# A build-time list scheduler with other durations, latencies and filler rule, and score maxima in passes of three or four heads

## The chip, the cores and the metric

The kernel runs on one core of one Trainium2 chip. The metric is the device time in microseconds of one execution; medians are over several runs. TensorE is called PE here (PEld is its weight load), VectorE DVE, ScalarE ACT, GpSimd POOL, and SyncE, which issues the DMAs, SP.

## The reference

Four layers work in sequence on x of shape (8, 256, 32, 32), float32. Cut to what matters:

```python
# layer 0: attention, 4 heads of width 32 (values 64), then a gated feed-forward with 8x8 FFTs
attn = softmax(einsum('bhkn,bhkm->bhnm', q, k) * SCALE)           # 1024 x 1024 per head
out  = einsum('bhdm,bhnm->bhdn', v, attn) + dwconv3(v)
x    = x + gamma1 * proj(out);  x = x + gamma2 * edffn(ln(x))
# layer 1: group norm, attention with 8 heads of width 32, small MLP
attn = softmax(einsum('bhdi,bhdj->bhij', q, k) * temp)
# layer 2: quantised bottleneck convolution, its output is a code of 0 to 255
# layer 3: four scan directions of a selective state space model, 512 channels, 16 states
h = h * exp(dt * A) + dt * B_t * u_t;   y = sum_n h * C_t
```

## The kernel before

The program has two stages, one after the other. `phase_a` computes layers 0 to 2 for the eight samples, up to three of them in flight. `phase_b` computes layer 3: 64 blocks (8 samples, 4 directions, 2 halves of 512 positions), in each 16 states, in each 4 chunks of 128 channels.

**The list.** In both stages the order of instructions on the engines is made when the program is built, by the class `_Order`. Each piece of work is a generator, a *strand*, with a rank. It yields either a condition, for which it waits, or one operation, or a list of operations of one engine that go together. `run` computes for the next operation of every strand the time at which it could start (`start`), takes the earliest (the lower rank at equal times), emits it and moves the engine's clock (`free`) on by the operation's assumed cost. The chip never sees these times: they only decide the order in which each engine's queue holds its instructions. Each engine then works its own queue in order, and waits where its data isn't there.

- `_Op` holds the assumed cost of an operation by engine, size and place. `landing` is the assumed time of a DMA.
- `blocks` names the pieces of a tile that an operation reads or writes. A tile with at most 512 elements per partition is cut in pieces of 64, a larger one in pieces of 512. Two operations that touch one piece are taken as dependent, if one of them writes.
- `LATENCY` is added where a result goes from one engine to another.
- `keep_dense` puts fillers in front of a PE operation: bf16 matmuls of a constant `minus` (line 277 of the profile) whose result nobody reads. It wants work of half of the last 3.4 us. Their number is limited by the room up to the time at which the PE operation can start, or up to 0.66 us after PE became free, whichever is later.

All emitted operations carry line 147 (`_Op.emit`) in the profile, so groups are told apart by tile names: `bank` is a PSUM bank of stage one (eight of them), `stats` holds the maxima, `exps` the exponentials of the attention, `da`, `dbu`, `db`, `h`, `py` and `pp` are tiles of stage two.

**The maxima.** The softmax needs the maximum and the sum of each row of scores before the exponentials are multiplied by the values. `maxima` does this for four heads at a time (once per sample in layer 0, twice in layer 1): 8 row tiles `t`, 2 halves `j` of the keys, 4 heads `h`, that is 64 score tiles of 128x512. One *pass* computes some of them: PE multiplies 32-row slices of q and k, one per head, each in its own group of 32 rows of the array and its own bank; then per head DVE reduces the bank to a negated maximum (`least`) and ACT exponentiates it with that bias and accumulates the sum (`sums`). `least` and `sums` are halves of one `stats` tile of 128 columns. Two strands (`MAXIMA`) work on one list of 32 entries, each for heads h and h+1. A strand takes four heads where four banks are free and the entry is that of head 0, and two otherwise.

**Banks.** `may(n)` tells whether n banks may be taken. While some attention is under way (`attending`), banks of other work (`lent`: maxima and projections alike) may be three at most (`OTHERS`).

**The attention proper.** `exponentials` runs for one sample at a time. A step computes the scores of four 128x512 tiles, subtracts the row terms with the `minus` matmuls, exponentiates on ACT, and a second strand multiplies with the values. `SCORES` is the assumed cost of the first list.

**Stage two.** Eight endless strands work side by side: `scales` (ACT, `dbu`), `turns` (PE transposes into `db`), `decays` (ACT exponentials, `da`), `scans` (DVE, `h`), `products` (POOL, times `cb`), `sums` (PE transposes into `py`), `rows` (SP loads of `cb`), `ahead` (the inputs of coming blocks: projections, convolutions, and in `tables` the batches of ACT functions that need another table). `da` has 5 buffers, `db` 3 banks, `h` 6, `cb` 3.

Of the kernel before, what the change touches and what calls it, by code (L numbers as in the profile page):

```python
# [20 lines left out]
F32 = mybir.dt.float32  # L21
U8 = mybir.dt.uint8
BF16 = mybir.dt.bfloat16
AF = mybir.ActivationFunctionType
ALU = mybir.AluOpType
AX = mybir.AxisListType
# [3 lines left out]
P = 128  # L30
# [3 lines left out]
NT = N // P  # L34
HALF = 512
# [64 lines left out]
class _Op:  # L100


    def __init__(self, engine, method, args, kw):
        self.engine, self.method, self.args, self.kw = engine, method, args, kw
        out, ins = args[0], [a for a in (*args[1:], *kw.values()) if isinstance(a, bass.AP)]
        self.reads = {k for a in ins for k in self.blocks(a)}
        self.writes = {k for a in (out, kw.get("accum_out")) if a is not None for k in self.blocks(a)}
        self.landing = 0.0
        n = max(math.prod(a.shape[1:]) for a in (out, *ins)) / 1024
        near = all(a.space == out.space and out.space != PSUM for a in ins)  # L110
        points = sum(math.prod(a.shape[1:]) == 1 for a in ins)
        if engine == "tensor":
            x = kw.get("rhs", ins[0])
            n = math.prod(x.shape[1:]) / 1024
            self.rows = x.shape[0] / P * n * (0.44 if x.dtype != F32 else 1.72)
            move = method == "transpose" or kw.get("is_transpose", False)
            self.cost = max(0.06, (0.22 if x.shape[0] < 20 else 0) + n * (0.96 if move else 0.44 if x.dtype != F32 else 1.76 if n > 0.2 else 2.0))
            self.rows *= 0.5 if move else 1
        elif engine == "vector":
            fast = near and method in ("tensor_scalar", "tensor_copy")  # L120
            both = near and method == "tensor_tensor"
            three = near and method == "scalar_tensor_tensor"
            if method == "tensor_tensor_scan":
                self.cost = 0.03 + 2.15 * n + 0.05 * points
            elif both or three:
                self.cost = 0.04 + 1.5 * n
            elif fast:
                self.cost = 0.04 + 0.9 * n
            else:
                self.cost = 0.05 + 1.09 * n + 0.05 * points  # L130
        elif engine == "scalar":
            self.cost = 0.05 + 0.06 * near + 0.85 * n + 0.093 * points + 0.17 * ("accum_out" in kw)
        elif engine == "gpsimd":
            self.cost = 0.12 + 2.2 * n if method == "tensor_tensor" else 0.07 + (2.0 if out.dtype == BF16 else 1.5) * n
        else:
            self.cost, self.landing = 0.1, 3.0

    @staticmethod
    def blocks(a):
        step = max(1, a.ap[0][0])  # L140
        lo = a.offset % step
        hi = lo + sum((n - 1) * abs(s) for s, n in list(a.ap)[1:])
        unit = 64 if step <= HALF else HALF
        return [(a.name, k) for k in range(lo // unit, hi // unit + 1)]

    def emit(self, nc):
# [37 lines left out]
class _Order:  # L184
# [2 lines left out]

    LATENCY = 0.35  # L190

    def __init__(self, nc):
        self.nc, self.strands, self.n = nc, [], 0
        self.free, self.written, self.read, self.base, self.last = {}, {}, {}, {}, {}
        self.rooms, self.minus, self.way, self.rows, self.fresh = [], None, 0.0, [], {}

    def add(self, rank, strand):
        self.n += 1
# [30 lines left out]

    def put(self, room, t):  # L230
        k = room.of[t.name]
        end = [v[0] for d in (self.written, self.read) for v in d.pop(t.name, {}).values()]
        self.last[room.tag, k] = max(end + [0.0]) + self.LATENCY
        room.put(t)

    def start(self, ops):
        e = ops[0].engine
        t = self.free.get(e, 0.0)
        for o in ops:
            for k in o.reads | o.writes:  # L240
                t = max(t, self.base.get(k[0], 0.0))
                w, by = self.written.get(k[0], {}).get(k, (0.0, e))
                t = max(t, w + (self.LATENCY if by != e else 0.0))
            for k in o.writes:
                w, by = self.read.get(k[0], {}).get(k, (0.0, e))
                t = max(t, w + (self.LATENCY if by != e else 0.0))
        return t

    WINDOW, DENSE, DUMMY = 3.4, 0.5, 0.22

    def keep_dense(self, t, cost, ops):

        work = sum(o.rows for o in ops)
        free, end = self.free.get("tensor", 0.0), t + cost
        self.rows = [r for r in self.rows if r[1] > end - self.WINDOW]
        seen = sum(w * (b - max(a, end - self.WINDOW)) / (b - a) for a, b, w in self.rows)
        n = math.ceil((self.DENSE * self.WINDOW - seen - work * min(1.0, self.WINDOW / cost)) / self.DUMMY)
        n = max(n, math.ceil((t - free - self.DENSE * self.WINDOW) / self.DUMMY))
        if n > 0:
            since, room, k = min(  # L260
                ((self.last.get((r.tag, k), 0.0), j, k) for j, r in enumerate(self.rooms) for k in r.left),
                default=(1e9, 0, 0),
            )
            x = self.fresh.get(ops[0].args[0].name)
            if x is not None and self.base[x.name] < since:
                since, room = self.base[x.name], None
            begin = max(free, since)
            n = min(n, int((max(t, free + 0.66) - begin) / self.DUMMY))
            if since < 1e9 and n > 0:
                if room is not None:  # L270
                    room = self.rooms[room]
                    room.left.remove(k)
                    room.left.insert(0, k)
                    x = room.take()
                rhs = self.minus.unsqueeze(1).to_broadcast([P, 4, P])
                for _ in range(n):
                    self.nc.tensor.matmul(x, lhsT=self.minus, rhs=rhs, start=True, stop=True)  # L277
                if room is not None:
                    room.put(x)
                    self.last[room.tag, k] = begin + n * self.DUMMY + self.LATENCY  # L280
                self.rows.append((begin, begin + n * self.DUMMY, n * self.DUMMY))
                t = max(t, begin + n * self.DUMMY)
        self.rows.append((t, t + cost, work))
        return t

    def run(self):
        while self.strands:
# [12 lines left out]
            cost, ops = s[2]  # L300
            e = ops[0].engine
            if self.rooms and e == "tensor":
                t = self.keep_dense(t, cost, ops)
            for o in ops:
                o.emit(self.nc)
                for k in o.reads:
# [9 lines left out]
def phase_a(ctx, tc, i, col, ident, codes, w_parts):  # L316
# [18 lines left out]
    order = _Order(nc)  # L335
    NBIG, NMID, NLOW = 12, 9, 7
    OTHERS = 3
    MAXIMA, SCORES = 2, 1.12
    GATE = 1
    big = _Room(rooms, "big", NBIG, [P, CC, N])  # L340
    mid = _Room(rooms, "mid", NMID, [P, N])
# [105 lines left out]
    def hs(h):  # L447
        return slice(h * HALF, (h + 1) * HALF)
# [4 lines left out]
    def may(n):  # L453

        return len(bank.left) >= n and (not attending or len(lent) + n <= OTHERS)
# [13 lines left out]
    def back(b):  # L469
        for t in b if isinstance(b, list) else [b]:  # L470
            lent.discard(t.name)
            put(bank, t)
# [110 lines left out]
    def maxima(rank, q, k, rows, done):  # L583

        both = yield from take(stats)
        least, sums = both[:, 0], both[:, 1]
        todo = [(t, j, h) for t in range(NT) for j in range(2) for h in (0, 2)]
        left = [MAXIMA]

        def some():  # L590
            while todo:
                yield lambda: not todo or may(2)
                if not todo:
                    break
                n = 4 if may(4) and not todo[0][2] else 2
                t, j, h = todo.pop(0)
                if n == 4 and todo:
                    todo.pop(0)
                bb = yield from some_banks(n)
                ops = []  # L600
                for e in range(n):
                    r = slice(32 * (h + e), 32 * (h + e) + 32)
                    ops.append(
                        T.matmul(bb[e], lhsT=q[r, t * P : (t + 1) * P], rhs=k[r, hs(j)], start=True, stop=True)
                    )
                yield (0.9, ops)
                for e in range(n):
                    m, s = (x[:, j, t, h + e : h + e + 1] for x in (least, sums))
                    yield V.tensor_reduce(m, bb[e], AX.X, ALU.max, negate=True)
                    yield A.activation(bb[e], bb[e], AF.Exp, bias=m, accum_out=s)  # L610
                    back(bb[e])
            left[0] -= 1

        for _ in range(MAXIMA):
# [491 lines left out]
        def emit(self, nc):  # L1106
            nc.scalar.preload_act_table_set("natural_log_exp_and_others")

    order.rooms, order.minus, order.way = [bank], minus, 0.05
    stage = [0] * B  # L1110

    def sample(b):
# [670 lines left out]
```

## Time and profile before

| | us |
|---|---|
| median of 3 runs | 10249.33 (10241.9 to 10274.5) |
| profiled execution | 10256.65 |
| its span, first to last instruction | 10254.8 |
| PE, PEld busy | 9573.8, 5920.9 |
| DVE, ACT, POOL busy | 7741.9, 8521.2, 6150.3 |
| granted clock of TensorE | 0.977 |

The profile shows one execution. A group of instructions is written as line, engine, operation, written tile <- read tiles, shapes, count; then busy time in us, mean ns of one, and the idle time of the engine just before them with what ended it. The maxima end at 3564 us and the last DMAs of stage one land near 3700 us; the change of stages shows in the table of 40 slices too, where POOL goes from 1 to 4 tenths to 7 and 8. A matmul of float32 leaves two records of PE, a transpose one. Busy PE is wider than the work in it, since the end of a matmul is modelled.

### The profile page before, as it was taken

Reading aid. Unit: us, or ns where it says so; the run is one execution under the profiler, and the core shown is the slowest. Engines: PE = TensorE matmul, PEld = TensorE weight load, DVE = VectorE, ACT = ScalarE, POOL = GpSimd, SP = SyncE. Lnnn points to the kernel's source line nnn. Section 1 sums busy time; section 2 is a strip of 40 time slices with the busy share of each in tenths; the row PEclk is TensorE's granted clock in tenths of the full one; section 3 lists DMA queues with packets and bytes.
Section 4 is the critical chain, followed back from the end, with each engine's and each line's share of the span. In section 5 each row is a group of like instructions: output and inputs, shape, how many; then the busy total and the mean of one; then the engine's idle time right before and its main releaser. Section 6 shows DMA issues by size and latency. Waiting matters only on the chain.

```text
span 10254.8 us, 153646 instructions
## 1 busy us (share of the span) xinstructions
PE 9573.8 (93%) x57349; PEld 5920.9 (58%) x57349; DVE 7741.9 (75%) x8671; ACT 8521.2 (83%) x15873; POOL 6150.3 (60%) x2993
## 2 busy tenths in 40 slices
PE   9999999999999989999999999999999999999998
PEld 3333333333333347777777777777777776777776
DVE  6366557585666448887888888888888888888788
ACT  7867676767666759988998999898999899898898
POOL 1433132242121038877887878787878787787788
PEclk9998999999999999999999999999999999999999
DMA  2100000000000002112111112111111211111111
GB/s 59 30 19 17 21 22 18 17 22 17 17 17 9 17 29 54 52 47 57 44 55 55 47 51 59 44 55 50 54 51 49 55 54 45 59 50 49 55 46 54
DMA packets 219630, 416.06 MB, mean 41 GB/s; under 512 B 25137, under 2 KB 67505, under 8 KB 213762
## 3 DMA queue, kind: packets, MB, share of 16 engines
q1 hardware_dynamic: 218882, 406.24, 13.7%
q8 instruction: 451, 7.39, 0.3%
q14 instruction: 297, 2.43, 0.1%
HBM read 358.43 MB, written 37.22 MB: 39 GB/s over the span
## 4 chain that ended last, share of the span: by engine, by line
ACT 28%; PE 22%; DVE 10%; issue 2%; POOL 1%; DMA 1%; DVEq 0%; SPq 0%; POOLq 0%; ACTq 0%
ACT da L147 11%; ACT dbu L147 10%; PE pp L147 9%; DVE h L147 8%; PE py L147 7%; PE db L147 6%; ACT L147 2%; ACT xs L147 1%; ACT dt L147 1%; DMA wi<-w_in 1%; POOL h L147 1%; ACT L156 1%; DVE ys L147 1%; ACT st L147 1%; ACT z L147 0%
## 5 line engine op out<-in xcount | busy, mean ns | idle before, releaser
L147 POOL TENSOR_TENSOR h<-h,cb 128x1024 f32<-128x1024 f32 x2048 | 4814.7, 2375 | 1013.8 <-DVE h L147 422.9
L147 ACT ACTIVATE da<-dt,am 128x512 f32<-128x512 f32 x4096 | 2863.9, 714 | 506.0 <-DVE h L147 502.0
L147 ACT ACTIVATE dbu<-du,bT 128x512 f32<-128x512 f32 x4096 | 2783.4, 709 | 17.1 <-PE db L147 10.4
L147 DVE TENSOR_TENSOR_SCAN h<-da,db 128x512 f32<-128x512 f32 x2048 | 2342.4, 1202 | 467.1 <-ACT da L147 201.5
L147 DVE TENSOR_TENSOR_SCAN h<-da,st,db 128x512 f32<-128x512 f32 x2048 | 2466.0, 1262 | 224.8 <-ACT da L147 131.3
L147 PE MATMUL db<-ident,dbu 128*128 128x128 f32 x16384 | 2329.7, 276 | 194.7 <-DVE h L147 157.7
L147 PEld LDWEIGHTS db<-ident,dbu 128*128 128x128 f32 x16384 | 1855.6, 141 | 798.8 <-DVE h L147 350.4
L147 PE MATMUL py<-ident,h 128*128 128x128 f32 x16384 | 2099.2, 274 | 95.4 <-POOL h L147 90.0
L147 PEld LDWEIGHTS py<-ident,h 128*128 128x128 f32 x16384 | 1837.4, 141 | 236.4 <-POOL h L147 179.2
L147 DVE TENSOR_REDUCE stats<-bank 128x1 f32<-128x512 f32 x1536 | 987.9, 684 | 655.0 <-PE bank L147 652.2
L147 ACT ACTIVATE bank<-bank,stats 128x512 f32<-128x512 f32 x1536 | 1024.7, 672 | 409.2 <-DVE stats L147 395.3
L147 POOL TENSOR_TENSOR mid<-mid,mid 128x961 f32<-128x961 f32 (+2 forms) x192 | 394.6, 2062 | 1115.5 <-ACT mid L147 591.9
L147 PE MATMUL bank<-big,big 32*128 32x512 f32 x4096 | 928.3, 667 | 15.7 <-ACT bank L147 9.0
L147 ACT ACTIVATE exps<-bank 128x512 f32<-128x512 f32 x1536 | 796.9, 620 | 166.4 <-PE bank L147 158.9
L147 PE MATMUL pp<-xi,cvd 128*128 128x512 f32 x1488 | 692.6, 601 | 1.6 <-DVE ys L147 1.6
L277 PEld LDWEIGHTS <-minus 128*128 128x128 bf16 x2805 | 260.6, 101 | 663.4 <-issue 463.8
L147 DVE SCALAR_TENSOR_TENSOR mid<-mid,cols,mid 128x961 f32<-128x961 f32 (+1 forms) x384 | 595.6, 1551 | 6.1
L277 PE MATMUL bank<-minus 128*128 128x512 bf16 x1749 | 508.5, 414 | 52.5 <-ACT bank L147 41.1
L147 PEld LDWEIGHTS bank<-big,big 32*128 32x128 f32 x4096 | 283.2, 191 | 463.0 <-issue 267.4
L147 PE MATMUL bank<-exps,big 128*32 128x512 f32 (+1 forms) x3072 | 543.8, 613 | 0.3 <-ACT exps L147 0.3
L147 POOL TENSOR_TENSOR tmp<-dt,xs 128x512 f32<-128x512 f32 x256 | 322.6, 1274 | 298.2 <-ACT dt L147 227.0
L147 POOL TENSOR_TENSOR big<-big,mid 128x992 f32<-128x992 f32 (+1 forms) x128 | 324.4, 2542 | 290.1 <-ACT mid L147 287.4
(207 smaller groups left out, 9389.5 us busy)
## 6 DMA issues: line engine op xcount, KB each, us to landing
cb<-c_d SPq DMA_DIRECT2D x1024, 256.0 KB, 3.3
wi<-w_in SPq DMA_DIRECT2D x192, 192.0 KB, 3.6
big<-in_x_dram SPq DMA_DIRECT2D x16, 1024.0 KB, 5.2
kept<-big SPq DMA_DIRECT2D x16, 1024.0 KB, 3.9
big<-kept SPq DMA_DIRECT2D x16, 1024.0 KB, 4.8
xf<-codes SPq DMA_DIRECT2D x48, 256.0 KB, 4.0
big<-big SPq DMA_DIRECT2D x16, 512.0 KB, 6.7
codes<-low SPq DMA_DIRECT2D x32, 256.0 KB, 2.0
```

Source lines behind the costliest of these rows:

```text
L147: return getattr(getattr(nc, self.engine), self.method)(*self.args, **self.kw)
L156: nc.scalar.preload_act_table_set("natural_log_exp_and_others")
L277: self.nc.tensor.matmul(x, lhsT=self.minus, rhs=rhs, start=True, stop=True)
```

## The change

It has four parts. The durations and landing in `_Op` get other constants, and a term for few-row matmuls goes. `blocks` cuts tiles of at most 256 elements per partition in single columns. `LATENCY` becomes a number by engine of the producer. Fillers may only fill the time before the planned start, and a new method `advance` follows windows of 3.4 us: after a window with less than 0.375 of work the list takes PE at half speed, so that the cost of a PE operation depends on when it runs. The maxima become one strand that takes the next three or four of 64 entries of one head each (the remaining ones at the end), instead of two strands with fixed pairs. `SCORES` and the overhead of a list on PE in stage one (`way`) get other values.

```diff
@@ _Op
-            self.rows = x.shape[0] / P * n * (0.44 if x.dtype != F32 else 1.72)
+            self.rows = x.shape[0] / P * n * (0.427 if x.dtype != F32 else 1.707)
             move = method == "transpose" or kw.get("is_transpose", False)
-            self.cost = max(0.06, (0.22 if x.shape[0] < 20 else 0) + n * (0.96 if move else 0.44 if x.dtype != F32 else 1.76 if n > 0.2 else 2.0))
+            self.cost = max(0.05, n * (0.427 if x.dtype != F32 else 0.854 if move else 1.707))
...
             elif both or three:
-                self.cost = 0.04 + 1.5 * n
+                self.cost = 0.04 + 1.53 * n
             elif fast:
-                self.cost = 0.04 + 0.9 * n
+                self.cost = 0.04 + 0.87 * n
             else:
-                self.cost = 0.05 + 1.09 * n + 0.05 * points
+                self.cost = 0.05 + 1.12 * n + 0.06 * min(points, 1)
         elif engine == "scalar":
-            self.cost = 0.05 + 0.06 * near + 0.85 * n + 0.093 * points + 0.17 * ("accum_out" in kw)
+            self.cost = 0.04 + 0.054 * near + 0.852 * n + 0.093 * points + 0.1 * ("accum_out" in kw)
         elif engine == "gpsimd":
-            self.cost = 0.12 + 2.2 * n if method == "tensor_tensor" else 0.07 + (2.0 if out.dtype == BF16 else 1.5) * n
+            self.cost = 0.12 + 2.3 * n if method == "tensor_tensor" else 0.07 + (2.0 if out.dtype == BF16 else 1.5) * n
         else:
-            self.cost, self.landing = 0.1, 3.0
+            self.cost, self.landing = 0.06, 3.6
...
-        unit = 64 if step <= HALF else HALF
+        unit = 1 if step <= 256 else 64 if step <= HALF else HALF
@@ _Order
-    LATENCY = 0.35
+    LATENCY = {"tensor": 0.21, "vector": 0.12, "scalar": 0.14, "gpsimd": 0.1, "sync": 0.06}
...
-                t = max(t, w + (self.LATENCY if by != e else 0.0))
+                t = max(t, w + (self.LATENCY[by] if by != e else 0.0))
...
+    def advance(self, t, cost, work):
+        while True:
+            while self.window < int(t / self.WINDOW + 1e-9):
+                self.half = self.dense < 0.375 * self.WINDOW
+                self.window, self.dense = self.window + 1, 0.0
+            pace = 0.5 if self.half else 1.0
+            end = (self.window + 1) * self.WINDOW
+            part = min(cost, (end - t) * pace)
+            self.dense += work * part / cost if cost else 0.0
+            work -= work * part / cost if cost else 0.0
+            cost -= part
+            t += part / pace
+            if cost < 1e-6:
+                return t
+            t = end + 1e-6
@@ keep_dense
-            n = min(n, int((max(t, free + 0.66) - begin) / self.DUMMY))
+            n = min(n, int((t - begin) / self.DUMMY))
...
-                self.rows.append((begin, begin + n * self.DUMMY, n * self.DUMMY))
-                t = max(t, begin + n * self.DUMMY)
-        self.rows.append((t, t + cost, work))
-        return t
+                done = self.advance(begin, n * self.DUMMY, n * self.DUMMY)
+                self.rows.append((begin, done, n * self.DUMMY))
+                t = max(t, done)
+        end = self.advance(t, cost, work)
+        self.rows.append((t, end, work))
+        return t, end - t
@@ phase_a
-    MAXIMA, SCORES = 2, 1.12
+    MAXIMA, SCORES = 1, 1.29
@@ maxima
-        todo = [(t, j, h) for t in range(NT) for j in range(2) for h in (0, 2)]
+        todo = [(t, j, h) for t in range(NT) for j in range(2) for h in range(4)]
...
-                yield lambda: not todo or may(2)
+                yield lambda: not todo or may(min(3, len(todo)))
                 if not todo:
                     break
-                n = 4 if may(4) and not todo[0][2] else 2
-                t, j, h = todo.pop(0)
-                if n == 4 and todo:
-                    todo.pop(0)
+                n = min(len(todo), 4)
+                while not may(n):
+                    n -= 1
+                n = min(n, 4)
+                take_now, todo[:n] = todo[:n], []
                 bb = yield from some_banks(n)
...
-                yield (0.9, ops)
+                yield (0.96 if n > 2 else 1.06, ops)
...
-    order.rooms, order.minus, order.way = [bank], minus, 0.05
+    order.rooms, order.minus, order.way = [bank], minus, 0.1
```

More of the change, by code (lines that the diff above doesn't have):

```diff
@@ L195, in __init__ @@
         self.rooms, self.minus, self.way, self.rows, self.fresh = [], None, 0.0, [], {}
+        self.window, self.dense, self.half = 0, 0.0, False
     def add(self, rank, strand):
@@ L231, in put @@
         k = room.of[t.name]
-        end = [v[0] for d in (self.written, self.read) for v in d.pop(t.name, {}).values()]
-        self.last[room.tag, k] = max(end + [0.0]) + self.LATENCY
+        end = [v[0] + self.LATENCY[v[1]] for d in (self.written, self.read) for v in d.pop(t.name, {}).values()]
+        self.last[room.tag, k] = max(end + [0.0])
         room.put(t)
@@ L242, in start @@
                 w, by = self.written.get(k[0], {}).get(k, (0.0, e))
-                t = max(t, w + (self.LATENCY if by != e else 0.0))
+                t = max(t, w + (self.LATENCY[by] if by != e else 0.0))
             for k in o.writes:
                 w, by = self.read.get(k[0], {}).get(k, (0.0, e))
-                t = max(t, w + (self.LATENCY if by != e else 0.0))
+                t = max(t, w + (self.LATENCY[by] if by != e else 0.0))
         return t
     WINDOW, DENSE, DUMMY = 3.4, 0.5, 0.22
+    def advance(self, t, cost, work):
[13 more added lines that the diff above has]
+            t = end + 1e-6
     def keep_dense(self, t, cost, ops):
@@ L279, in keep_dense @@
                     room.put(x)
-                    self.last[room.tag, k] = begin + n * self.DUMMY + self.LATENCY
-                self.rows.append((begin, begin + n * self.DUMMY, n * self.DUMMY))
-                t = max(t, begin + n * self.DUMMY)
-        self.rows.append((t, t + cost, work))
-        return t
+                    self.last[room.tag, k] = begin + n * self.DUMMY + self.LATENCY["tensor"]
+                done = self.advance(begin, n * self.DUMMY, n * self.DUMMY)
[4 more added lines that the diff above has]
+        return t, end - t
     def run(self):
@@ L302, in run @@
             if self.rooms and e == "tensor":
-                t = self.keep_dense(t, cost, ops)
+                t, cost = self.keep_dense(t, cost, ops)
             for o in ops:
@@ L591, in some @@
             while todo:
-                yield lambda: not todo or may(2)
+                yield lambda: not todo or may(min(3, len(todo)))
                 if not todo:
                     break
-                n = 4 if may(4) and not todo[0][2] else 2
-                t, j, h = todo.pop(0)
-                if n == 4 and todo:
-                    todo.pop(0)
+                n = min(len(todo), 4)
[3 more added lines that the diff above has]
+                take_now, todo[:n] = todo[:n], []
                 bb = yield from some_banks(n)
                 ops = []
[L601 to L605, printed above, removed]
-                yield (0.9, ops)
[L607 to L611, printed above, removed]
+                for b, (t, j, h) in zip(bb, take_now):
+                    r = slice(32 * h, 32 * h + 32)
+                    ops.append(T.matmul(b, lhsT=q[r, t * P : (t + 1) * P], rhs=k[r, hs(j)], start=True, stop=True))
+                yield (0.96 if n > 2 else 1.06, ops)
+                for b, (t, j, h) in zip(bb, take_now):
+                    m, s = (x[:, j, t, h : h + 1] for x in (least, sums))
+                    yield V.tensor_reduce(m, b, AX.X, ALU.max, negate=True)
+                    yield A.activation(b, b, AF.Exp, bias=m, accum_out=s)
+                    back(b)
             left[0] -= 1
```

## The prediction

> **What bounds the kernel now.** I read the table of stretches first, because the kernel is two programs one after the other: the first 3640 us are the convolution and attention layers (stage one, the only stage with score maxima), the rest is the state-space scan (stage two).
>
> ```profile
> 0.00:3640.00 3640.00, 3455.60 (x15580) 1229.61 (x15581) 2172.65 (x3236) 2630.82 (x5717) 913.44 (x467) 0.94 0.07 21
> 3640.00:10255.00 6615.00, 6118.25 (x41770) 4691.30 (x41768) 5569.25 (x5436) 5890.40 (x10156) 5236.88 (x2526) 1.00 0.18 51
> ```
>
> The columns after the length are PE, weight loads, DVE, ACT, POOL, then the granted clock. In stage one PE is busy 95% of the time, ACT 72%, DVE 60%, and the clock is 0.94. In stage two ACT is busy 89%, DVE 84%, at full clock. So the stages have different limits and must be costed apart. Next the groups of PE by shape in stage one:
>
> ```profile
> L147 PE MATMUL bank<-big,big 32*128 32x512 f32 x4096 | 928.3, 667 | 15.7 <-ACT bank L147 9.0 <-ACT exps L147 4.1 <-DVE big L147 1.6
> L277 PE MATMUL bank<-minus 128*128 128x512 bf16 x1665 | 488.9, 416 | 52.5 <-ACT bank L147 41.1 <-ACT exps L147 4.1 <-DVE low L147 2.7
> L147 PE MATMUL bank<-big 32*128 32x512 f32 x2048 | 459.0, 657 | 14.3 <-DVE big L147 5.0 <-ACT exps L147 3.9 <-ACT bank L147 2.8
> ```
>
> The 32-row score matmuls are the largest work of PE, and 488.9 us of its busy time are fillers (L277) that compute nothing. A score matmul leaves two records. Half of these 6144 records belong to the maxima (1536 heads), half to the attention proper. Without fillers PE is busy about 2970 of 3640 us, 82%. The timeline of PE then shows what a pass costs:
>
> ```profile
> 1207.69 1.14 PE L147 MATMUL bank<-big,big 32*128 32x512 f32 x8
> 1208.76 1.98 PE L147 MATMUL bank<-big,w_qkv 128*128 128x512 f32 x4
> 1210.68 1.13 PE L147 MATMUL bank<-big,big 32*128 32x512 f32 x4
> 1211.74 0.39 PE L277 MATMUL bank<-minus 128*128 128x512 bf16 x1
> 1212.06 1.13 PE L147 MATMUL bank<-big,big 32*128 32x512 f32 x4
> 1213.12 1.98 PE L147 MATMUL bank<-big,w_qkv 128*128 128x512 f32 x4
> ```
>
> Four heads (x8) take 1.14 us, two heads (x4) take 1.13; from the start of either to the start of what follows is 1.06 us. A pass costs the same however many heads are in it. And DVE, beside the attention of the last sample:
>
> ```profile
> 3398.72 1.29 DVE L147 TENSOR_REDUCE stats<-bank 128x1 f32<-128x512 f32 x2 [6.04 <-PE bank L147]
> 3403.97 1.29 DVE L147 TENSOR_REDUCE stats<-bank 128x1 f32<-128x512 f32 x2 [3.97 <-PE bank L147]
> 3411.65 1.29 DVE L147 TENSOR_REDUCE stats<-bank 128x1 f32<-128x512 f32 x2 [6.38 <-PE bank L147]
> ```
>
> Two heads are reduced in 1.29 us, then DVE waits 4 to 6 us for the next pass. The waits of DVE in stage one put 652.2 us on this. For stage two the waits say that ACT and DVE hold each other up:
>
> ```profile
> ACT da L147 <- DVE h L147: 502.0, 421, 4.8
> DVE h L147 <- ACT da L147: 332.8, 69, 7.6
> DVE h L147 <- PE py L147: 180.4, 219, 3.9
> ```
>
> ACT waits 502 us for a scan to give a buffer back, DVE 333 us for the exponential that ACT has late behind its batches of tables, and 180 us behind PE work that was queued ahead.
>
> **What the Trainium skill says.** "TensorE: Matmul & The Clock Gate", section "Part 3: Packing small matmuls — row/col tiling", says that matmuls in different 32-row groups run together, four at 3.07 times the rate; here 1.14 against 1.13 us for twice the heads agrees. "TensorEngine Tiling (Array Packing)", section "PSUM Bottleneck", warns that emptying PSUM becomes the limit afterwards; here it isn't yet, as ACT is at 72%, but one head needs 0.68 us of DVE and 0.67 of ACT after its share of a pass. The page "TensorE: Matmul & The Clock Gate", section "What's actually happening", has the clock at half rate after an idle window of about 3.4 us; the 0.94 above fits short dips.
>
> **The change part by part.**
>
> *Passes.* Counted in the program, the maxima of before are 670 passes of two and 49 of four: 719 passes. After, a pass takes the next three or four heads of the list whatever their place, so it is between 1536/4 = 384 and 1536/3 = 512 passes. Three holds beside attention (at most three lent banks), four otherwise; I take the middle, 448. That removes 719 - 448 = 271 passes of 1.06 us, **287 us** of PE (219 to 355). The reduces and exponentials, 1536 each, stay. With PE occupied 82% by real work and DVE waiting on it, I put all of it on the path.
>
> *The false chain in the order.* The list takes all 64 columns of the minima as one block (unit 64), so it believes that a reduce must wait until the exponential of another head has read its bias, and adds 0.35 us each time. The trace doesn't have that wait (the stats group waits 25.5 us on ACT, all told), so it costs nothing directly, but it spaces the maxima in the order that the queues must follow. After, each column is its own block. Two strands per pass become one: of these the second covered the time in which the first emptied its banks. I set the gain of the one against the loss of the other, at -80 to +80 us, value 0.
>
> *Fillers.* The old rule lets a group of fillers push a ready matmul by up to 0.66 us, the new one not. Replaying the rule on the kernel before, 68 of 474 groups in stage one do so, 100 of 1749 fillers. At 488.9/1665 = 0.294 us each that is **29 us**; the rest stand in gaps that remain. If most of those gaps are only believed (latency 0.35 against 0.1 to 0.2), up to 150 us more; if the clock falls from 0.94 to 0.91 instead, 3% of 2970 us, 89 us are lost. The three together: value 29.
>
> *Costs and latencies, stage one.* SCORES goes from 1.12 to 1.29, against 0.96 + 0.33 us in the trace between the starts of scores, minus and values. This only places other work better; nothing, bounded by 50 us either way, since it sits inside the attention whose PE work is unchanged.
>
> Stage one: 287 + 29 = 316, taken as **-320 us**, from 3640 to 3320. ACT's 2631 us would then be 79% of it, so ACT doesn't stop it yet.
>
> *Stage two.* No instruction is added or removed but fillers (290 us busy, in a stage where PE isn't the bound). The list's durations come nearer: a 128-column transpose 0.12 to 0.107, where four are 0.47 us apart in weight loads; an exponential 0.628 to 0.613, where two follow at 0.61. Work is then queued on PE less far ahead of the scans. The waits at stake are 502 + 333 + 180 us; a tenth of them, minus what new orders put elsewhere, gives **-60 us**. ACT and DVE alternate, so the sum can't be gained twice. Bounds: -220 (ACT from 89% to 92%) and +130 (2% of 6615), since a greedy order can also come out worse with truer numbers.
>
> Queues: SP's loads keep their places relative to their users except where landing 3.6 instead of 3.0 moves them earlier; the next user waits on three buffers of cb, so zero. POOL's order in stage one changes with ACT's; it is at 25% there, and is covered.
>
> Sum: -320 - 60 = -380 us. The profiled execution took 10256.65 us (span 10254.8), 7.3 above the median of 10249.33. From the median: **9870 us**.
>
> **The rivals.** *A, the passes weren't the path.* Each sample's chain of maxima, attention and projections, or ACT, holds stage one; emptied banks come no faster, and only a third of the PE time shows: 316/3 = 105, stage two 0: 10145 us. For it: ACT waits 409.2 us before the maxima's exponentials, mostly for DVE, not PE. Against: DVE's 652.2 us on PE.
>
> *B, starved maxima (the slower side).* Beside attention a pass of three needs all three lent banks at once, so any projection that holds one bank blocks it, where a pass of two let one stand beside it. A projection holds its bank for about 1.98 + 0.6 = 2.6 us (four records and the copy). With half of the heads beside attention there are 768/3 = 256 such passes; the gain of 380 us is gone at 380/256 = 1.5 us of added wait each, on the path. At 2.6 us it is 666 - 380 = +286: 10535 us. For it: one strand only, and no second one to fill in. Against: maxima rank ahead of projections when banks come free, and passes beside attention are 5 to 8 us apart already.
>
> *C, stage two goes the wrong way.* +130 there and -105 in stage one: 10275 us, about even.
>
> *D, the change does less than it says.* Fewer passes, but still 512 of three, and slower clock: 219 - 89 = -130: 10120 us. It goes with A.
>
> **How the numbers follow.** The forecast, with its bounds, has 0.62; A and D 0.22; B 0.08; C 0.08. A change within 0.3% (31 us) is about what this kernel's measurement cannot tell from none. Of C, 0.03 lies within it and 0.05 above; all of B is slower. So faster 0.84, same 0.03, slower 0.13. The low end: 355 + 100 in stage one and 200 in stage two, 655, gives 9595; I take 9600. The upper end takes in A and D and stops at 10200, leaving out B, C and little else.
>
> **What would show it.** Right: PE rows of x6 and x8 in place of x4, 384 to 512 passes, stage one ending near 3320 us, fewer than 1665 fillers, DVE's wait for PE in the stats group well under 652 us, the clock at 0.92 or more. Stage two: ACT's wait for scans under 502 us and a length of 6500 to 6600. Wrong: stage one over 3550 us with DVE waiting 6 us or more for a pass of three (B); PE at 85% with ACT over 80% (A); stage two over 6650 (C).

## The result and the profile after

The changed kernel takes 10080.6 us (median of 4 runs, 10077.1 to 10083.6) against 10259.5 us of the kernel before in the same comparison: ratio 0.9826, 95% interval 0.9807 to 0.9845. It gains 179 us, 1.7%. The forecast was 380 us. The profiled execution has a span of 10079.9 us, 174.9 less than before.

In every kernel of this study I take stage one to end with the last multiplication by the values, which the view of the tile `exps` gives (minimum, median and maximum in ns, then first and last start in us). Of the changed kernel:

```profile
L147 PE MATMUL bank<-exps,big x3072: 592/592/1117, 175.7 to 3481.0; 128*32 128x512 f32 x128, 128*64 128x512 f32 x64
```

That is 3481.0 us; before it was 3635.6. So stage one became 154.6 us shorter (forecast 320), and stage two, 6619.2 before and 6598.9 after, 20.3 us (forecast 60). The table of stretches, columns as before:

```profile
0.00:3485.00 3485.00, 3256.31 (x15144) 1222.19 (x15145) 2255.23 (x3230) 2610.13 (x5722) 942.48 (x472) 0.95 0.07 22
3485.00:10080.00 6595.00, 6066.05 (x41512) 4707.40 (x41632) 5570.53 (x5436) 5901.83 (x10156) 5238.02 (x2526) 0.99 0.17 51
```

In stage one ACT's work (2610 us) is what it was and its share rose to 75%; the clock is 0.95. Stage two has the same work in nearly the same time. PE's groups in stage one:

```profile
L147 PE MATMUL bank<-big,big 32*128 32x512 f32 x4096 | 845.0, 650 | 14.4 <-ACT bank L147 8.4 <-ACT exps L147 3.3 <-ACT low L147 2.2
L147 PE MATMUL bank<-big 32*128 32x512 f32 x2048 | 422.9, 664 | 19.3 <-DVE big L147 8.9 <-ACT exps L147 4.9 <-ACT bank L147 4.3
L295 PE MATMUL bank<-minus 128*128 128x512 bf16 x1230 | 340.3, 403 | 24.3 <-ACT bank L147 14.5 <-ACT low L147 6.8 <-POOL eps L387 1.6
```

The score matmuls lost 119 us of busy time (928.3 + 459.0 before), the fillers (now line 295) 149 us. The group of DVE's reduces:

```profile
L147 DVE TENSOR_REDUCE stats<-bank 128x1 f32<-128x512 f32 x1536 | 972.0, 681 | 400.7 <-PE bank L147 394.2
```

DVE waits 394 us for passes, 258 less than before. The passes themselves, in PE's timeline:

```profile
1343.50 1.13 PE L147 MATMUL bank<-big,big 32*128 32x512 f32 x6
1344.56 5.42 PE L147 MATMUL bank<-big,w_qkv 128*128 128x512 f32 x12
1349.91 1.14 PE L147 MATMUL bank<-big,big 32*128 32x512 f32 x8
1350.98 0.66 PE L147 MATMUL bank<-ident,big 128*128 128x128 f32 x4
1351.47 1.24 PE L295 MATMUL bank<-minus 128*128 128x512 bf16 x5
1352.65 2.03 PE L147 MATMUL bank<-big,big 32*128 32x512 f32 x8
```

Three heads (x6) and four (x8) cost 1.13 and 1.14 us, as two did, but the last pass of four takes 2.03. ACT's timeline beside it tells why:

```profile
1352.59 0.25 ACT L147 ACTIVATION_READ_ACCUMULATOR bank<-bank,stats 128x1 f32 x1
1352.68 0.70 ACT L147 ACTIVATE bank<-bank,stats 128x512 f32<-128x512 f32 x1
1353.25 0.25 ACT L147 ACTIVATION_READ_ACCUMULATOR bank<-bank,stats 128x1 f32 x1
```

ACT is done with two banks of the pass before at 1352.84 and 1353.50; the weight loads of the third and fourth head start at 1352.89 and 1353.55. PE stands in the middle of the pass until each bank is emptied, and what is queued behind it stands too. I call a pass split if its matmuls start in more than two groups (all first records together, then all second ones, are two). Of the 458 passes some 270 are split, of the 719 before some 75. Last, the waits of stage two (who waited <- for whom: us in all, how often, longest):

```profile
ACT da L147 <- DVE h L147: 444.3, 392, 5.6
DVE h L147 <- ACT da L147: 335.2, 70, 6.4
DVE h L147 <- PE py L147: 185.5, 176, 4.3
```

ACT waits 58 us less for scans; DVE waits as before.

### The profile page after: what moved, and what is told of

It reads as the page before. It is cut to its first block, busy times and chain, and to the rows that moved or that the text cites. A ratio compares the mean times of both kernels' runs of the same rounds, so it can differ in the third digit from the quotient of the medians.

```text
span 10079.9 us, 152800 instructions
## 1 busy us (share of the span) xinstructions
PE 9322.4 (92%) x56655; PEld 5929.6 (59%) x56777; DVE 7825.8 (78%) x8666; ACT 8512.0 (84%) x15878; POOL 6180.5 (61%) x2998
## 4 chain that ended last, share of the span: by engine, by line
PE 28%; ACT 22%; DVE 11%; issue 3%; DMA 1%; POOL 1%; DVEq 0%; SPq 0%; POOLq 0%; ACTq 0%
PE pp L147 12%; DVE h L147 9%; ACT da L147 9%; PE py L147 8%; PE db L147 8%; ACT dbu L147 7%; ACT L147 2%; ACT xs L147 2%; ACT dt L147 1%; DMA wi<-w_in 1%; ACT L156 1%; DVE du L147 1%; POOL h L147 1%; ACT st L147 0%; DVE ys L147 0%
## 5 line engine op out<-in xcount | busy, mean ns | idle before, releaser
L147 PE MATMUL db<-ident,dbu 128*128 128x128 f32 x16384 | 2400.5, 278 | 390.2 <-DVE h L147 336.1
L147 PE MATMUL bank<-big,big 32*128 32x512 f32 x4096 | 845.0, 650 | 14.4 <-ACT bank L147 8.4
L147 DVE SCALAR_TENSOR_TENSOR mid<-mid,cols,mid 128x961 f32<-128x961 f32 (+1 forms) x384 | 629.2, 1639 | 5.9
L147 PE MATMUL bank<-exps,big 128*32 128x512 f32 (+1 forms) x3072 | 565.2, 627 | 0.7 <-ACT exps L147 0.6
L147 POOL TENSOR_SCALAR big<-big,ga,gs 128x512 f32<-128x512 f32 x64 | 74.5, 1176 | 750.6 <-DVE gs L147 292.5
L147 POOL TENSOR_TENSOR big<-big,mid 128x961 f32<-128x961 f32 (+1 forms) x128 | 326.2, 2556 | 302.1 <-ACT mid L147 279.9
L295 PEld LDWEIGHTS <-minus 128*128 128x128 bf16 x2233 | 210.0, 101 | 446.7 <-issue 263.2
```

The costliest lines, as they stand in the source:

```text
L147: return getattr(getattr(nc, self.engine), self.method)(*self.args, **self.kw)
```

## The experiments

Each kernel is the changed one (*after*) or the one before with the edit named. Ratios are to the kernel before on the same chip; its median was 10253 to 10276 us there. Stage lengths come from one profiled execution of each kernel. Where an edit leaves a stage as it was, its length moves by 1 to 4 us (e1 and e13 against *after*).

| | edit | median us | ratio (95%) | stage one | stage two |
|---|---|---|---|---|---|
| before | | 10259.5 | 1 | 3635.6 | 6619.2 |
| after | | 10080.6 | 0.9826 (0.9807 to 0.9845) | 3481.0 | 6598.9 |
| e1 | after, maxima in pairs | 10086.5 | 0.9830 (0.9815 to 0.9845) | 3483.3 | 6599.9 |
| e2 | before, maxima in threes and fours | 10220.8 | 0.9961 (0.9945 to 0.9976) | 3596.9 | 6622.4 |
| e3 | after, banks free later | 10076.6 | 0.9819 (0.9800 to 0.9837) | 3485.7 | 6595.4 |
| e4 | after, old filler rule | 10098.9 | 0.9841 (0.9826 to 0.9857) | 3493.9 | 6602.1 |
| e5 | after, old pieces of 64 columns | 10092.9 | 0.9836 (0.9818 to 0.9853) | 3490.5 | 6607.6 |
| e6 | after, latency 0.35 for all | 9935.1 | 0.9682 (0.9667 to 0.9698) | 3448.9 | 6483.9 |
| e7 | after, old durations | 10294.4 | 1.0036 (1.0024 to 1.0048) | 3535.3 | 6755.9 |
| e8 | after, latency of DVE 0.35 | 9964.8 | 0.9710 (0.9690 to 0.9730) | 3448.3 | 6510.2 |
| e9 | after, 0.35 for all but DVE | 9993.5 | 0.9736 (0.9717 to 0.9755) | 3414.8 | 6580.2 |
| e10 | after, latency 0.5 for all | 9926.7 | 0.9671 (0.9649 to 0.9694) | 3449.9 | 6474.8 |
| e11 | e6, maxima in pairs | 9926.6 | 0.9673 (0.9654 to 0.9692) | 3439.4 | 6483.4 |
| e12 | after, latency of e9 in stage one, of e10 in stage two | 9888.8 | 0.9635 (0.9618 to 0.9651) | 3411.8 | 6476.2 |
| e13 | after, old PE durations in stage two | 10197.9 | 0.9935 (0.9918 to 0.9952) | 3485.1 | 6711.9 |
| e14 | after, old ACT durations | 10131.1 | 0.9868 (0.9848 to 0.9889) | 3498.1 | 6636.9 |

The first question was whether the passes or the list's numbers brought the gain.

**e1, the new list with the old maxima.**

```diff
-    MAXIMA, SCORES = 1, 1.29
+    MAXIMA, SCORES = 2, 1.29
-        todo = [(t, j, h) for t in range(NT) for j in range(2) for h in range(4)]
+        todo = [(t, j, h) for t in range(NT) for j in range(2) for h in (0, 2)]
...
-                yield (0.96 if n > 2 else 1.06, ops)
+                yield (0.9, ops)
```

> The changed kernel, with only the maxima put back as before (two strands, pairs of heads, 0.9 assumed per list). Theory P (the passes brought the gain, by taking less PE time): PE's time in maxima goes back from 700 us to about 830, the end of stage one moves from 3481 us to about 3610, total about 10210 us. Theory L (the truer durations, latencies and single-column blocks of the list brought it): stage one stays at 3440 to 3520, total 10040 to 10120. Stage two is the same program in both, 6600 us within 10.

Theory P is refuted: 682 passes in place of 458, and stage one is 2 us longer. PE in stage one of this kernel:

```profile
L147 PE MATMUL bank<-big,big 32*128 32x512 f32 x4096 | 900.9, 658 | 7.3 <-ACT bank L147 4.8 <-ACT low L147 1.2 <-DVE big L147 1.2
L295 PE MATMUL bank<-minus 128*128 128x512 bf16 x1048 | 303.9, 406 | 38.4 <-ACT exps L147 22.9 <-ACT bank L147 12.9 <-POOL eps L387 1.6
```

Adding up the time from each PE record's start to the next one's, the maxima hold PE for 770 us here and 700 in the changed kernel; some 37 of the 70 us are taken out of fillers (364 against 401 us), the rest out of the time that other work holds PE.

**e2, the old list with the new maxima.** The same lines the other way round, in the kernel before.

> The kernel before, with only the maxima changed (one strand, passes of three or four of any next heads); the list's numbers as before. Theory P: stage one about 145 us shorter than before, total about 10110 us. Theory L: no gain, 10230 us or more, since one strand alone in a list that believes each reduce must wait for the exponential of the head before works the maxima off more slowly. Stage two 6620 us as before.

Between the two: 39 us shorter in stage one. PE in stage one of this kernel:

```profile
L147 PE MATMUL bank<-big,big 32*128 32x512 f32 x4096 | 797.8, 640 | 10.1 <-ACT bank L147 9.4 <-DVE low L147 0.6
L277 PE MATMUL bank<-minus 128*128 128x512 bf16 x2251 | 580.3, 397 | 52.8 <-ACT bank L147 40.3 <-ACT exps L147 5.1 <-ACT low L147 4.9
```

The score matmuls are shorter than in the changed kernel (797.8 against 845.0), and stage one is 116 us longer; the list has put fillers (580.3 us) where the saved time was. With e1, where PE has more work and the stage is as long, this says that PE's load isn't the bound of stage one.

**e3, banks believed free later.**

```diff
             self.cost = 0.04 + 0.054 * near + 0.852 * n + 0.093 * points + 0.1 * ("accum_out" in kw)
+            self.landing = 0.4 * ("accum_out" in kw)
```

> The changed kernel; the list takes a bank of the maxima to come free 0.3 to 0.4 us later than it did. Theory S (the passes of three and four cost 1.7 to 2.1 us where they are split, because PE stands in the middle of the pass until ACT has emptied the third or fourth bank): split passes fall from 266 to under 130, PE's time in maxima from 700 to about 570 us, total 9950 to 10030 us. Rival W (the wait only moves to other work of PE, ACT sets the pace of the maxima in any case): fewer split passes, total 10060 us or more.

This put neither theory to the test. Of the passes, 232 are still split, where it was some 270, and the maxima take PE 700 us as before; so the total, which is in W's range, does not tell what the absence of splits would be worth. Only the setting's own effect is known: none.

**e4, the old filler rule.**

```diff
-            n = min(n, int((t - begin) / self.DUMMY))
+            n = min(n, int((max(t, free + 0.66) - begin) / self.DUMMY))
```

> The changed kernel with the old rule on fillers (up to 0.66 us after PE became free). If the forced fillers cost little, as the prediction had it: 0 to 30 us slower, 10080 to 10110. If the new rule was a main part of the gain: 10160 to 10200 us. If fewer fillers cost clock: faster than 10060 us with a clock over 0.975.

13 us in stage one, 3 in stage two: as small as expected, and no larger than what the medians of the kernel before differ by between chips.

The second set takes the list's numbers apart.

**e5, the old pieces.**

```diff
-        unit = 1 if step <= 256 else 64 if step <= HALF else HALF
+        unit = 64 if step <= HALF else HALF
```

> The changed kernel with the old cutting of tiles (pieces of 64 columns), so that the list again takes each reduce of a sample's maxima to wait for the exponentials read before it. Theory B (the false chain in the order was the main brake of stage one): stage one back to 3580 to 3640 us, total 10190 to 10250. Theory N (as the prediction valued it, near nothing): within 30 us of the changed kernel, 10050 to 10110. Stage two is unchanged within 15 us in both, 6599.

Theory N: 9.5 us in stage one. The false chain was worth next to nothing with one strand. What the fine pieces are worth in the kernel before, and the coarse ones with the maxima in pairs, is not known: the list finds no order for them.

**e6, the old latency.**

```diff
-    LATENCY = {"tensor": 0.21, "vector": 0.12, "scalar": 0.14, "gpsimd": 0.1, "sync": 0.06}
+    LATENCY = dict.fromkeys(("tensor", "vector", "scalar", "gpsimd", "sync"), 0.35)
```

> The changed kernel with 0.35 us of latency for every engine in the list. Theory T (the shorter latencies were the main part): 10170 us or more, most of it in stage one; stage two some 20 us longer. If durations or blocks were the main part: within 40 us of the changed kernel.

Neither side: the sign is the other one. With 0.35 us the kernel is 145 us faster, 32 in stage one and 115 in stage two. The new latencies cost time.

**e7, the old durations in `_Op`.** The lines of the diff from `self.rows` to `landing`, undone.

> The changed kernel with the old assumed durations of single operations (the exponential with its sum again 0.83 us in the list where ACT takes 0.66, transposes and float32 matmuls longer). Theory C (truer durations were the main part): 10170 us or more. Otherwise within 40 us of the changed kernel. In stage two, where the list's PE work grows by a tenth with this, the changed kernel's 20 us would be gone, if they came from the durations: 6620 instead of 6599 us.

Theory C, and more: 214 us slower, 54 in stage one and 157 in stage two. With the short latencies and the old durations the kernel is slower than before. So two large effects of opposite sign stood behind the small change of stage two. Step by step from the kernel before: with everything new but the latencies (e6) stage two is 135 us shorter, and the new latencies then add 115, which leaves the 20. The other way round, with everything new but the durations (e7) it is 137 us longer, and the durations then take off 157. ACT's group of exponentials in stage two, of e7 and then of e6, shows where:

```profile
L147 ACT ACTIVATE da<-dt,am 128x512 f32<-128x512 f32 x4096 | 2874.6, 714 | 616.6 <-DVE h L147 605.2
```

```profile
L147 ACT ACTIVATE da<-dt,am 128x512 f32<-128x512 f32 x4096 | 2867.4, 714 | 332.8 <-DVE h L147 327.3
```

Same work; the idle time before it, until a scan gives its buffer back, is 605 us and 327. Over the kernels this wait and stage two go together, if not strictly: 327 us and 6484, 335 and 6510 (e8), 424 and 6580 (e9), 444 and 6599 (after), 451 and 6637 (e14), 502 and 6619 (before), 605 and 6756 (e7), 610 and 6712 (e13). Between e7 and e6 278 us of wait stand against 272 us of stage. ACT's work is nearly the same in all of them, so a longer stage has to show as idle time of ACT; the list of waits tells where on ACT it lies, not what causes it.

**e8, e9, the latency of DVE alone, and of all others.**

```diff
+    LATENCY = {"tensor": 0.21, "vector": 0.35, "scalar": 0.14, "gpsimd": 0.1, "sync": 0.06}
```

> The changed kernel with 0.35 us of latency for DVE's results alone, the others as changed. Theory V (what hurts is that the list takes a scan's result too early: it counts 1.225 to 1.275 us from its start to its user, the trace shows 1.295): stage two falls from 6599 to 6500 us or less, as with 0.35 for all (6484), total 9980 or less. Theory M (a margin on every hand-over keeps the order loose against drift): less than half of the 115 us come, stage two over 6540.

```diff
+    LATENCY = {"tensor": 0.35, "vector": 0.12, "scalar": 0.35, "gpsimd": 0.35, "sync": 0.35}
```

> The complement: 0.35 us for PE, ACT, POOL and SP, 0.12 for DVE. Theory V: stage two stays within 30 us of 6599. Theory M: stage two 6484 to 6560, the greater part of the 115 us.

Stage two goes by theory V: 89 of the 115 us come with DVE's latency, 19 with the others'. It came to 6510, 10 us over the limit written down. Stage one doesn't follow: 33 us with DVE's, 66 with the others', 32 with both. I take this for the scatter of single orders, some 30 us there, and read no cause from differences of that size. In stage two the short latency of DVE shows on ACT's timeline. The changed kernel:

```profile
5019.88 0.71 ACT L147 ACTIVATE dbu<-du,bT 128x512 f32<-128x512 f32 x1
5020.92 0.72 ACT L147 ACTIVATE da<-dt,am 128x512 f32<-128x512 f32 x1 [0.33 <-DVE h L147]
5022.03 0.20 ACT L147 COPY st<-h 128x2 f32<-128x2 f32 x1 [0.39 <-DVE h L147]
```

and e6, in the same stretch of time:

```profile
5032.30 0.71 ACT L147 ACTIVATE dbu<-du,bT 128x512 f32<-128x512 f32 x1
5032.91 0.71 ACT L147 ACTIVATE da<-dt,am 128x512 f32<-128x512 f32 x1
5033.53 0.71 ACT L147 ACTIVATE dbu<-du,bT 128x512 f32<-128x512 f32 x1
5034.14 0.18 ACT L147 COPY st<-h 128x2 f32<-128x2 f32 x1
```

Where ACT's queue holds a `da` or a copy that comes a little before its scan is over, ACT stands 0.3 to 0.4 us; in e6 it goes from one to the next. Behind the copy at 5022.03 stood a `da` that was free to start since 5021.65; behind the `da` at 5020.92 nothing was ready. DVE runs without a gap through this stretch, so the lines show the wait and not what it costs.

**e10, 0.5 us for all.** The line of e6 with 0.5.

> The changed kernel with 0.5 us of latency for all engines. Theory M: like 0.35, stage two 6450 to 6520, total 9900 to 9970. If 0.35 were a lucky order of a greedy list and nothing more: anywhere between 6480 and 6620, as likely as not above 6550.

As theory M has it: 6475, no worse than 0.35. Up to 0.5 us, the longest tried, too long a latency costs stage two nothing.

**e11, e6 with the maxima in pairs.** The edits of e1 and e6 together.

> The changed kernel with 0.35 us of latency for all and the maxima of before (two strands, pairs). If passes of three and four are worth something once the order is loose: stage one 3480 us or more, where it is 3449 with them, total over 9965. If they are worth nothing, as with the short latencies: stage one 3420 to 3470, total 9910 to 9955. Stage two is the same program as with 0.35 and passes of three and four, 6484.

Worth nothing here either: stage one is 9.5 us shorter with pairs.

**e12, latencies by stage.** One line in `phase_a`, one in `phase_b`, each after `order = _Order(nc)`:

```diff
+    order.LATENCY = {"tensor": 0.35, "vector": 0.12, "scalar": 0.35, "gpsimd": 0.35, "sync": 0.35}
+    order.LATENCY = dict.fromkeys(("tensor", "vector", "scalar", "gpsimd", "sync"), 0.5)
```

> The changed kernel with 0.35 us of latency for all but DVE (0.12) in stage one and 0.5 us for all in stage two. The stages are independent programs one after the other, so their lengths should simply add: 3415 + 6475 = 9890 us of span, total about 9892 us, 3.6% under the kernel before and 1.9% under the changed kernel. If the stages are not independent (the end of one sets the start of the other): anything up to 9935.

9888.8 us: the stages add. This is the fastest kernel here, 3.65% under the one before. Its latencies for stage one are the best of those tried there, picked after the fact; no run shows why they are.

**e13, e14, whose durations.** In e13 `_Op` uses the old formula for PE once stage two begins; in e14 only ACT's line is the old one.

> The changed kernel, with the old assumed durations of PE's operations in stage two alone (a 128-column transpose 0.12 in place of 0.107, a float32 matmul of 512 columns 0.88 in place of 0.854). Theory E (the list's PE was too slow against its ACT, so it queued transposes early and other work late): most of the 157 us of the kernel with all old durations come back, stage two 6700 us or more, ACT's wait for scans over 550. Rival A (ACT's durations did it): stage two within 40 us of 6599.

> The changed kernel with the old assumed durations of ACT's operations (stage two: 0.628 in place of 0.613 for each exponential and each scaling; stage one: the exponential with its sum 0.83 in place of 0.75, where it takes 0.66). Rival A: stage two 6700 us or more, stage one about 3535 as with all old durations. Theory E: stage two within 40 us of 6599; stage one takes the 54 us that all old durations cost there, 3520 to 3540.

Theory E for stage two: PE's durations account for 113 of the 157 us, ACT's for 38. ACT's wait in e13:

```profile
L150 ACT ACTIVATE da<-dt,am 128x512 f32<-128x512 f32 x4096 | 2868.2, 714 | 617.3 <-DVE h L150 610.4
```

In stage one theory E missed: ACT's durations account for 17 of 54 us, and the other 37 are not divided.

## Why the prediction was right or wrong

**The bound of stage one** was misread, and with it the largest term failed: "With PE occupied 82% by real work and DVE waiting on it, I put all of it on the path." The count was right (458 passes where 448 were taken). The price was not: a pass that isn't split costs about 1.0 to 1.1 us in the mean, but some 270 of the 458 are split by waits for banks, at about 1.7 us for three heads and 2.1 for four. The maxima gave 146 us of PE back instead of 287. The Trainium skill's "TensorEngine Tiling (Array Packing)", section "PSUM Bottleneck", which says that emptying PSUM may become the bottleneck, and which the prediction set aside with ACT's 72%, fits the trace here: the emptying of the banks came to set the pace inside the pass, long before ACT's share was high (75%). And even the 146 us weren't on the path: e1 and e11 show passes of two as fast. The change of the maxima, 287 us in the sum, is worth 39 us at most in the runs here (e2). The total still lies between the 9600 and 10200 us named; as far as the passes go that is luck, since e1 gets there without them.

That PE's busy time is elastic could have been seen: fillers were 488.9 us of it, and the list puts them wherever PE has nothing to do. The wait of DVE for PE (652 us) was a wait for the order of PE's queue, not for PE's throughput: in e11, with 721 passes, DVE waits 386 us. What does bound stage one is not shown.

**The false chain**, 0 within 80 us, held: 9.5 us (e5). **Fillers**, 29 us: e4 shows 13 + 3. The fall of the clock, feared at 89 us, didn't come (0.94 to 0.95).

**Durations and latencies of stage one**, "nothing, bounded by 50 us either way": the bounds nearly held (54 us gained by the durations, 32 lost by the latencies), but these are no smaller than the terms that I counted. The parts measured by taking each out of the changed kernel, 54 + 13 + 10 + 2 - 32, make 47 us, not 154, and all but the first are about as small as the scatter of single orders. Three parts of the change were taken out in no run: `SCORES`, `way` and the half speed of `advance`. Whether the other 107 us are theirs, or the parts replace one another, stays open.

**Stage two**, -60: the sign was right by luck, the step was wrong. To take "a tenth of them", of the waits, made of durations and latencies one small effect. They are two large ones: -157 and +115 us where each is taken out of the changed kernel, with -135 for all that is new but the latencies and +137 for all but the durations. The argument "The list's durations come nearer" was right, and PE the right place to look (e13, which doesn't part transposes from other matmuls). In the trace, transposes that follow one another in stage two start 0.109 us apart (median), so 0.107 is nearer than 0.12; the 0.47 us for four that the prediction read would have spoken for 0.12. I gave the durations less than half of their size. The latencies were priced at nothing of their own in stage two, and cost 115 us or more.

Are the new latencies too short, or just too near? I paired in the changed kernel's stage two each instruction that started at its release with what released it. After a scan that begins from zero, PE transposes start 1.25 us (median) after the scan's start, and exponentials 1.25; the list counts 1.225. After one that begins from a kept state it is 1.31 and 1.29; the list counts 1.275. For an ACT scaling to PE it is 0.76 against 0.753. So DVE's hand-over is 0.02 to 0.04 us too short in the list and ACT's is right, which agrees with e8 and e9. An exact value for DVE (0.14 to 0.16) wasn't tried, so error and lack of margin are not told apart below 0.35; above, e10 shows that margin is free in stage two.

**The rivals.** B, starved maxima, didn't come: beside the last sample's attention DVE's reduces run on end,

```profile
3309.99 35.39 DVE L147 TENSOR_REDUCE stats<-bank 128x1 f32<-128x512 f32 x53
```

53 of them, back to back. A was right that the passes weren't the path, and its 10145 is nearer than 9870. Its reason, each sample's chain or ACT, was tested in no run; ACT is at 75%, not over 80 as A's sign had it. C's loss in stage two exists (+115), covered by a gain that it didn't have.

## What to carry to other kernels

Where a planner fills idle time of an engine with dummy work, that engine's busy time says little of a bound: take out the fillers, and even then ask whether a kernel with less work on it (e2) is shorter. Of a planner's assumed numbers, nearer durations helped here (e7), and latencies did better on the long side (e6, e10): one believed too long cost nothing that showed up to 0.5 us. The reading that fits is that in queues worked in order a result that comes even 0.02 to 0.04 us later than planned stops everything behind its user; no run shows it apart from a lack of margin. And when several numbers change at once, cost each by itself, with its own sign: -135 and then +115 looked like -20.

## What the runs showed of the hardware

From the end of the releasing instruction to the start of the waiting one the changed kernel's trace shows 0.03 to 0.06 us in stage two: 0.054 from a scan to PE, 0.034 from a scan to ACT, 0.052 from ACT to PE (medians). An exponential with a sum holds its bank for 0.78 us (median; 0.83 in the mean), though the next one starts 0.66 us after it, because the read of the accumulator follows it. And a pass of row-packed matmuls whose third bank is late doesn't let later work by: PE stands, for some 0.6 us with three heads and 1.0 with four on average (1.7 and 2.1 against 1.07).
